# Routing tokens to experts: one threshold ahead of the experts, seven in steps between their matmuls

## The chip, the cores and the metric

The kernel runs on one core of one Trainium2 chip. The metric is the device time of one launch in microseconds (us), the median of the runs. The core has five engines with queues of their own, each working through its instructions in order: PE (TensorE, matmul, with its weight loads shown as PEld), DVE (VectorE), ACT (ScalarE), POOL (GpSimd) and SP (which here only issues DMAs). An engine waits for another only through semaphores.

## The reference, cut to what matters

The reference is two transformer layers over 4096 tokens of width 256. The last block, a mixture of eight experts, is the one that matters here. Each expert chooses its own tokens: the 1024 with the highest scores.

```python
n = b * l                                   # 4096 tokens
k = min(max(int(n * C / e), 1), n)          # 1024 of them for each of e = 8 experts
S = jax.nn.sigmoid(xt @ Wg).T               # scores, expert by token
G, I = jax.lax.top_k(S, k)
ex = xt[I]
hid = jax.nn.gelu(jnp.einsum('ekh,ehf->ekf', ex, W1) + b1[:, None, :], approximate=False)
out = (jnp.einsum('ekf,efh->ekh', hid, W2) + b2[:, None, :]) * G[..., None]
new_x = jnp.zeros_like(xt).at[I.reshape(-1)].add(out.reshape(-1, h))
```

Here `e` is 8, `h` 256 and the hidden width 1024. The input `xt` is a layernorm of what the attention block before it leaves, and a layernorm of `new_x` is added to that at the end.

## The kernel before, in words

The kernel runs four stages in turn: a gated attention layer with its feed forward, a 16-head attention with ReLU weights, the routing, and the experts. In all stages the order of PE, DVE and ACT work is written out by hand (`manual_schedule`); POOL and SP are ordered by the framework until expert 6, from where POOL is by hand too.

**The end of the attention.** The last two tiles of 128 tokens are closed by `at_once` (L1249 to L1278), a chain of small steps on DVE: output projection, three layernorms, the transposes for the router (`turn_gating`, L1203) and the router matmul (`gate`, L1216), whose result is added to `logits` (L1233). `logits` has 128 partitions, 16 segments of 256 tokens by 8 experts, and 256 columns, the tokens of a segment. Loops of matmuls on nothing (`keep_busy`, L203) stand where PE would otherwise be idle.

**The routing (L1462 to L1564).** The sigmoid of all logits is taken at once (L1468 to L1471). Two transposes and eight DMAs put the scores beside the tokens' rows in DRAM (L1478 to L1486, `tok_d`). Then all eight thresholds are searched together, bit by bit: 15 rounds of two bits each (L1497 to L1524). In a round, DVE compares the 256 scores of a partition with three candidates and counts (L1501, with an accumulator), one small matmul adds the counts of an expert's segments (L1505), and three short DVE steps choose the next candidates (L1509, L1516, L1520). From the thresholds a mask, a tie rule and two running sums give every chosen token its place in its expert's list (L1527 to L1564): the chunk `hi` and the place in the chunk `lo`.

**The lists (class `List`).** For an expert, `chunks` (L1577) and four `places` (L1591) turn `hi` and `lo` into zero-one matrices on DVE, four `collect` (L1601, eight matmuls each) multiply them to the list of token numbers, and `gather` (L1615) folds it to indices and issues eight indirect DMAs on POOL (`fetch`, L1626) that bring the rows of the chosen tokens, 128 each.

**The experts (`feed_forward`, L1805).** Each expert is done in two units of 512 tokens, so u = 0 to 15. A unit has eight steps f (hidden blocks: matmuls L1819 and a gelu on ACT, L1826) and four steps i (output tiles: matmuls L1842, DVE steps L1859 and L1860, a scatter with addition on POOL, L1861). After i = 1 and i = 2 the next unit's tokens are transposed (`turn`, L1790, evacuated by DVE, L1803). Unit 0 does the f steps in two halves of 256 tokens. In the first unit of each expert the next expert's list is made: `chunks` after f = 1, `places` after f = 2 to 5, all four `collect` ahead of the i steps, and `gather` after i = 0. The list of expert 0 is made ahead of unit 0 (L1874 to L1880), and 15 empty matmuls follow its `gather`.

## Time and profile before

| what | us |
|---|---|
| median of 3 runs (1625.87 to 1626.36) | 1626.24 |
| the profiled execution, its own time | 1625.33 |
| its span, first to last instruction | 1623.5 |
| PE busy | 1562.3 (96%) |
| DVE busy | 904.9 (56%) |
| ACT busy | 647.6 (40%) |
| POOL busy | 402.0 (25%) |
| attention and router end, last addition to `logits` | at 1089.5 |
| first round of the search to the threshold | 1093.3 to 1122.9 |
| first matmul of expert 0 | at 1141.8 |
| one unit of an expert without, with a list to make | 28.4, 30.7 |

"Busy" is time in which an engine worked on an instruction; a busy PE may be one that works on nothing (`keep_busy`). A row of the timeline has the start in us from the span's start, the duration, the engine, the line of the kernel, the operation, what it writes from what, the shape, and in brackets the idle time of the engine before it and what ended it. The chain of waits is followed back from the last instruction, at each step to what released it.

### The profile page before, as it was taken

The numbers are of one execution on the slowest core, as the hardware profiler recorded it, in microseconds if no ns is written. First come the engines' busy times: TensorE is split into PE (matmuls) and PEld (weight loads), VectorE is DVE, ScalarE is ACT, GpSimd is POOL, SyncE is SP. The second block draws the span as 40 slices with busy tenths as digits, with TensorE's granted clock in tenths as the row PEclk, the third lists the DMA queues.
The fourth block names the chain that finished last, engine by engine and source line by source line (L and its number), as shares of the span: only waits on it lengthen the run. The fifth ranks groups of instructions, "written<-read, shape, count | busy, mean of one in ns | idle before, by whom it ended". The sixth has DMA issues, their size and how long they took to land.

```text
span 1623.5 us, 23583 instructions
## 1 busy us (share of the span) xinstructions
PE 1562.3 (96%) x9270; PEld 797.6 (49%) x9270; DVE 904.9 (56%) x2080; ACT 647.6 (40%) x1115; POOL 402.0 (25%) x436
## 2 busy tenths in 40 slices
PE   7999999999999999999999999983999999999997
PEld 3666666666322223232323224541757667566574
DVE  5555565664657787878787787767211212222145
ACT  3344444544544545454544455641221121211233
POOL 4122232222201011111101010110424324324555
PEclk9999999999999999999999999996999999999999
DMA  8300000000000000101010100031233233233355
GB/s 205 121 1 1 1 1 1 0 1 1 1 1 1 11 31 7 34 1 40 1 40 1 36 4 27 28 129 30 57 75 70 66 75 72 66 75 88 67 146 140
DMA packets 70090, 71.22 MB, mean 44 GB/s; under 512 B 23613, under 2 KB 62938, under 8 KB 69850
## 3 DMA queue, kind: packets, MB, share of 16 engines
q1 hardware_dynamic: 56096, 47.01, 9.4%
q0 software_dynamic: 13008, 21.77, 7.4%
q8 instruction: 73, 1.20, 0.3%
q10 hardware_dynamic: 874, 0.93, 0.2%
q14 instruction: 39, 0.32, 0.1%
HBM read 41.74 MB, written 27.95 MB: 43 GB/s over the span
## 4 chain that ended last, share of the span: by engine, by line
PE 92%; DVE 3%; issue 2%; POOL 1%; ACT 1%; DMA 0%; POOLq 0%; SPq 0%; ACTq 0%; DVEq 0%
PE sc L1303 17%; PE po L1329 16%; PE ph L1819 13%; PE py L1842 13%; PE py L799 4%; PE pg L691 4%; PE pv L707 3%; PE ph L855 2%; PE po L771 2%; PE pt L1145 2%; PE pv L380 2%; PE pq L356 2%; PE pq L876 2%; PE po L775 2%; PE pk L356 2%
## 5 line engine op out<-in xcount | busy, mean ns | idle before, releaser
L1312 ACT ACTIVATE w<-sc 128x512 f32<-128x512 f32 x512 | 277.9, 594 | 218.5 <-PE sc L1303 101.7
L1317 DVE TENSOR_SCALAR w<-sc 128x1024 f32<-128x1024 f32 x240 | 293.2, 1222 | 99.2 <-PE sc L1303 71.1
L1303 PE MATMUL sc<-qT,kT 32*128 32x512 f32 (+1 forms) x2304 | 294.7, 586 | 1.5 <-ACT w L1312 0.8
L1329 PE MATMUL po<-w,vaug 128*17 128x512 f32 (+1 forms) x2304 | 276.1, 550 | 1.0 <-ACT w L1315 0.3
L1842 PE MATMUL py<-w,hid 128*128 128x256 f32 x1024 | 230.1, 380 | 0.0
L1826 ACT ACTIVATE hid<-ph,mb 128x512 f32<-128x512 f32 (+1 forms) x136 | 90.1, 662 | 344.4 <-PE ph L1819 343.7
L1819 PE MATMUL ph<-xT,w 128*128 128x512 f32 (+1 forms) x544 | 222.8, 567 | 0.7 <-DVE xT L1803 0.7
L1842 PEld LDWEIGHTS py<-w,hid 128*128 128x128 f32 x1024 | 191.1, 190 | 32.0 <-issue 7.0
L1303 PEld LDWEIGHTS sc<-qT,kT 32*128 32x128 f32 x2304 | 94.4, 183 | 173.9 <-issue 157.9
L1819 PEld LDWEIGHTS ph<-xT,w 128*128 128x128 f32 x544 | 103.2, 190 | 111.1 <-issue 107.6
L1329 PEld LDWEIGHTS po<-w,vaug 128*17 128x17 f32 x2304 | 44.8, 95 | 191.5 <-issue 157.5
L1861 POOL DMA_INDIRECT acc_d<-y,idx x56 | 88.2, 1574 | 156.1 <-issue 127.0
L1628 POOL DMA_INDIRECT got<-tok_d,idx x64 | 65.9, 1030 | 152.3 <-DVE idx L1618 135.2
L1859 DVE TENSOR_TENSOR y<-py,mb 128x256 f32<-128x256 f32 x56 | 23.4, 419 | 142.3 <-PE py L1842 135.9
L1803 DVE COPY xT<-tp 128x512 f32<-128x512 f32 (+1 forms) x34 | 22.3, 660 | 91.6 <-PE tp L1798 91.6
L1067 POOL TENSOR_TENSOR rsg<-veg,mhalf 128x1 f32<-128x1 f32 x30 | 16.7, 555 | 205.0 <-DVE veg L1066 205.0
L691 PE MATMUL pg<-nT,wh 128*128 128x512 f32 x128 | 60.8, 607 | 1.5 <-ACT nT L630 1.5
L799 PE MATMUL py<-wo,oT 128*128 128x256 f32 x256 | 61.9, 385 | 0.0
L707 PE MATMUL pv<-wh,nT 128*128 128x512 f32 x128 | 59.7, 592 | 0.0
L1618 DVE CAST idx<-parts 128x8 int32<-128x8 f32 x8 | 1.3, 167 | 101.8 <-PE parts L1616 101.8
L799 PEld LDWEIGHTS py<-wo,oT 128*128 128x128 f32 x256 | 47.3, 190 | 17.2 <-issue 9.4
L572 POOL TENSOR_TENSOR x<-x,y 128x1024 f32<-128x1024 f32 x14 | 32.9, 2351 | 73.3 <-ACT y L561 73.3
(295 smaller groups left out, 1933.3 us busy)
## 6 DMA issues: line engine op xcount, KB each, us to landing
w<-in_L_ffn_W_dram SPq DMA_DIRECT2D x16, 1024.0 KB, 5.2
x<-in_L_attn_x_dram SPq DMA_DIRECT2D x8, 512.0 KB, 4.0
acc_d<-logits SPq DMA_DIRECT2D x8, 512.0 KB, 5.1
tok_d<-hg SPq DMA_DIRECT2D x32, 128.0 KB, 1.7
x_d<-x SPq DMA_DIRECT2D x7, 512.0 KB, 2.9
back_w<-acc_d SPq DMA_DIRECT2D x6, 512.0 KB
out_dram<-x SPq DMA_DIRECT2D x20, 128.0 KB, 1.7
out_dram<-back_w POOLq DMA_DIRECT2D x4, 512.0 KB
```

The costliest lines, as they stand in the source:

```text
L691: nc.tensor.matmul(pg, lhsT=wh[:, c, HID + e * P : HID + (e + 1) * P], rhs=d["nT"][:, c, :], start=(c == 0), stop=(c == DC - 1),)
L707: nc.tensor.matmul(pv, lhsT=d["nT"][:, c, i * P : (i + 1) * P], rhs=wh[:, c, 0:HID], start=(c == 0), stop=(c == DC - 1),)
L799: nc.tensor.matmul(py, lhsT=d["oT"][:, e, :], rhs=wo[:, e, :], start=(e == 0), stop=(e == EC - 1))
L1303: nc.tensor.matmul(sc[:, m * n : (m + 1) * n], lhsT=row["kT"][t][rows, r, (kt + m) * P : (kt + m + 1) * P], rhs=row["qT"][rows, t, q0 : q0 ...
L1312: nc.scalar.activation(w[:, j, :], sc, AF.Relu)
L1317: nc.vector.tensor_scalar(w[:, 2:4, :], pair, 0.0, None, ALU.max)
L1329: nc.tensor.matmul(po[32 * j : 32 * j + HD + 1, weighed(halves, r)], lhsT=row["v"][:, kt + m, HQ * t + 2 * j + r, :], rhs=w[:, j, m * n : ...
L1628: return nc.gpsimd.indirect_dma_start(out=dst, out_offset=None, in_=rows[:, :], in_offset=self.at_chunk(c), bounds_check=NT - 1, oob_is_er ...
L1819: nc.tensor.matmul(ph, lhsT=w1[:, c, f * P : (f + 1) * P], rhs=xT[u][:, c, h * n : (h + 1) * n], start=(c == 0), stop=(c == DC - 1),)
L1826: nc.scalar.activation(hid[:, f, h * n : (h + 1) * n], ph, AF.Gelu, bias=mb1[:, e * FC + f : e * FC + f + 1])
L1842: nc.tensor.matmul(py, lhsT=hid[:, f, i * P : (i + 1) * P], rhs=w2[:, f, :], start=(f == 0), stop=(f == FC - 1),)
L1861: scatter = nc.gpsimd.indirect_dma_start(out=acc_d[:, :], out_offset=lists[e].at_chunk(k), in_=y, in_offset=None, bounds_check=NT - 1, oob ...
```

## The change

**Scores with tokens on partitions.** In `at_once`, ahead of the last router matmul, the logits of the first 30 tiles are transposed on PE, cut at -87 by DVE into `score_t` (128 partitions by 32 tiles by 8 experts, in the memory of `logits`), and their sigmoid is taken while the last tiles are still being normalized. One DMA stores those scores. The last router result is copied, transposed and made scores by itself, 16 columns wide, and stored by a second DMA.

**One search ahead, the others in steps.** A class `Search` holds the search for some experts at n bits a round. A `compare` is, per expert and candidate, one DVE comparison with accumulator over the 32 scores that a partition holds of that expert. A `tick` is the counting matmul (with a matrix of ones), the choice of the next candidates, and the next `compare`. Expert 0 is searched ahead of the experts at two bits (15 ticks). Experts 1, 2, (3, 4) and (5, 6, 7) are searched at three bits, 10 ticks each with 7 comparisons per expert.

**The places per expert.** `List.rank` takes the place of L1527 to L1564 for one expert: 13 short DVE steps and two matmuls, 32 or 64 columns wide.

**The order.** All steps of the searches and lists after the first stand in an agenda, each with the DVE time that it is reckoned to take and the earliest unit. After each f step and each i step of an expert one entry at most is issued, when what was issued before is reckoned to be done but for 0.3 us. Three entries (the first comparisons and two ticks of expert 1) are issued ahead of unit 0. `keep_busy` after the search and the lists goes from 13, 12 and 15 matmuls to 8 and 4; 13 behind the sigmoid are dropped.

```diff
@@ at_once
-                keep_busy(idle, 4)
+                tokens = side([P, SEG // P, P], "tokens")
+                for k in range(SEG // P):
+                    nc.tensor.transpose(tokens[:, k, :], logits[:, k * P : (k + 1) * P], ident)
+                keep_busy(idle, 3)
...
+                for k in range(SEG // P):
+                    nc.vector.tensor_scalar(
+                        score_t.rearrange("p (b z k) e -> p k z b e", b=B, k=SEG // P)[:, k],
+                        tokens[:, k, :].rearrange("p (z b e) -> p z b e", b=B, e=NE),
+                        -87.0, None, ALU.max,
+                    )
+                known = score_t[:, 0 : NTILE - SEG // P]
+                nc.scalar.activation(known, known, AF.Exp, scale=-1.0)
...
-                gate()
+                nc.vector.tensor_scalar(known, known, 1.0, None, ALU.add)
+                nc.vector.reciprocal(known, known)
+                score_rows = tok_d.rearrange("(j p) d -> p j d", p=P)[:, :, D : D + NE]
+                nc.sync.dma_start(score_rows[:, 0 : NTILE - SEG // P], known)
+                pg, rows = gate()
+                last_logits = wk.tile([P, SEG], F32, tag="y", name="last_logits")
+                nc.vector.tensor_copy(last_logits[rows, :], pg[rows, :])
...
+                new = score_t[:, NTILE - SEG // P : NTILE]
+                nc.vector.tensor_scalar(new, tokens[:, :, 32 - NE : 32], -87.0, None, ALU.max)
+                nc.scalar.activation(new, new, AF.Exp, scale=-1.0)
+                nc.vector.tensor_scalar(new, new, 1.0, None, ALU.add)
+                nc.vector.reciprocal(new, new)
+                nc.sync.dma_start(score_rows[:, NTILE - SEG // P : NTILE], new)
@@ class Search
+            def compare(self, r):
+                for i, e in enumerate(self.es):
+                    for k in range(1, self.v):
+                        ge = wk.tile([P, NTILE], F32, tag="ge", name="ge")
+                        nc.vector.tensor_scalar(
+                            ge, score_t[:, :, e], self.tried[:, i, k : k + 1], None, ALU.is_ge, ALU.add,
+                            accum_out=self.counts[:, r % 2, i, k : k + 1],
+                        )
+            def tick(self, r):
...
+                nc.tensor.matmul(pn, lhsT=all_b, rhs=counts, start=True, stop=True)
...
+                        nc.vector.scalar_tensor_tensor(kept, pn, float(TOPK), self.tried, ALU.is_ge, ALU.mult)
...
+                        nc.vector.tensor_reduce(best, kept, AX.X, ALU.max)
+                        nc.vector.tensor_tensor(
+                            tried.bitcast(I32),
+                            best.bitcast(I32).unsqueeze(2).to_broadcast([P, g, v]),
+                            now.unsqueeze(1).to_broadcast([P, g, v]),
+                            ALU.bitwise_or,
+                        )
...
+                    self.compare(r + 1)
...
+            def steps(self, behind=0):
+                g = len(self.es)
+                spent = 0.19 * g * (self.v - 1)
+                return [
+                    (spent, behind, lambda: self.compare(0)),
+                    *((spent + 0.6 + 0.1 * g, behind, lambda r=r: self.tick(r)) for r in range(self.rounds)),
+                ]
@@ class List
+            def steps(self):
+                behind = max(QPE * self.e - 3, 0)
+                return [
+                    (2.9, behind, self.rank),
+                    (1.2, behind, self.chunks),
+                    (1.4, behind, lambda: (self.places(0), self.places(1))),
+                    (1.4, behind, lambda: (self.places(2), self.collect(0), self.places(3), self.collect(1))),
+                    (0.3, behind, lambda: (self.collect(2), self.collect(3))),
+                    (0.3, behind + 1, self.gather),
+                ]
@@ feed_forward
-                    if coming is not None and h == TB // n - 1:
-                        if f == 1:
-                            coming.chunks()
-                        elif 2 <= f < 6:
-                            coming.places(f - 2)
+                    go_on_with_lists(u, 1.75 if u else 0.87)
...
+                go_on_with_lists(u, 1.9)
@@ ahead of the units
-        lists[0].chunks()
-        for part in range(4):
-            lists[0].places(part)
-            lists[0].collect(part)
-        lists[0].gather()
+        searches = [Search(*what) for what in (((0,), 2), ((1,), 3), ((2,), 3), ((3, 4), 3), ((5, 6, 7), 3))]
+        agenda = []
+        for search in searches[1:]:
+            agenda.extend(search.steps())
+            for e in search.es:
+                agenda.extend(lists[e].steps())
+        left = [0.0]
+        def go_on_with_lists(u, time):
+            left[0] = max(left[0] - time, 0.0)
+            if agenda and left[0] < 0.3 and agenda[0][1] <= u:
+                spent, _, step = agenda.pop(0)
+                left[0] += spent
+                step()
         first = ps.tile([P, TB], F32, tag="mm", name="idle", bufs=3)
-        keep_busy(first, 15)
+        for n, (_, _, step) in enumerate(searches[0].steps() + lists[0].steps()):
+            step()
+            if n == 0:
+                nc.vector.memset(parts[:, 0 : P + NC], 0.0)
+            if step == lists[0].rank:
+                keep_busy(first, 8)
+        for _ in range(3):
+            agenda.pop(0)[2]()
+        keep_busy(first, 4)
```

The constants made in the first stage (`later_constants`) change with it: about as many short DVE steps as before.

## The prediction

> **What bounds the kernel.** I read the chain of waits first: where is the end set, and does the routing lie on it? The page's shares say PE, and the chain in order of time says what a unit of an expert costs.
>
> ```profile
> PE 92%; DVE 3%; issue 2%; POOL 1%; ACT 1%; DMA 0%; POOLq 0%; SPq 0%; ACTq 0%; DVEq 0%
> ```
>
> ```profile
> 1187.60 6.91 PE py L1842 x32
> ...
> 1216.02 1.94 PE parts L1604 x30
> 1217.96 3.65 PE py L1842 x16
> 1221.62 3.56 PE py L1842 x16
> ```
>
> In the experts PE never waits, so every PE instruction put there costs its own time. Two output tiles take 6.91 us; with a list they take 3.65 + 3.56 = 7.21.
>
> Second, the timeline around the routing. Between the last addition to the logits and expert 0's first matmul, 52.2 us, PE has almost nothing real to do and DVE is the chain. The reader is to see the start-to-start times: comparison to comparison 0.40, round to round (1095.22 to 1097.18) 1.96, threshold to `chunks` 7.43, `chunks` to the first expert matmul 11.34.
>
> ```profile
> 1089.53 0.43 DVE L1233 TENSOR_TENSOR logits<-logits,pg 32x256 f32<-32x256 f32 x1 [2.37 <-PE pg L1224]
> ...
> 1093.27 0.48 DVE L1501 TENSOR_SCALAR_CACHE_REDUCE ge<-sc,bits 128x256 f32<-128x256 f32 x1
> ...
> 1095.22 0.48 DVE L1501 TENSOR_SCALAR_CACHE_REDUCE ge<-sc,tried 128x256 f32<-128x256 f32 x1
> 1095.63 0.08 DVE L1501 DVE_READ_ACCUMULATOR ge<-sc,tried 128x1 bf16 x1
> 1095.63 0.47 DVE L1501 TENSOR_SCALAR_CACHE_REDUCE ge<-sc,tried 128x256 f32<-128x256 f32 x1
> ...
> 1096.43 0.17 DVE L1509 TENSOR_TENSOR grown<-tried,bits 128x16 int32<-128x16 int32 x1
> 1096.57 0.16 PE L1505 MATMUL pn<-counts,same_b 128*128 128x4 bf16 x1 [1.79 <-DVE ge L1501]
> 1096.77 0.17 DVE L1516 SCALAR_TENSOR_TENSOR kept<-pn,grown 128x16 f32<-128x16 f32 x1 [0.17 <-PE pn L1505]
> 1096.98 0.17 DVE L1520 TENSOR_REDUCE tried<-kept 128x4 f32<-128x16 f32 x1
> 1097.18 0.48 DVE L1501 TENSOR_SCALAR_CACHE_REDUCE ge<-sc,tried 128x256 f32<-128x256 f32 x1
> ...
> 1122.99 0.48 DVE L1530 TENSOR_SCALAR_CACHE_REDUCE mask<-sc,thr 128x256 f32<-128x256 f32 x1
> ...
> 1130.42 0.43 DVE L1579 TENSOR_TENSOR which<-hi,count_c 128x256 bf16<-128x256 bf16 x1
> ...
> 1135.37 0.17 DVE L1618 CAST idx<-parts 128x8 int32<-128x8 f32 x1 [1.46 <-PE parts L1616]
> ```
>
> Third, the windows (window, length, busy time and count of PE, PEld, DVE, ACT, POOL, then granted clock): when does PE's clock fall, and how much room has DVE in a unit?
>
> ```profile
> 1094.00:1096.00 2.00, 0.16 (x1) 0.10 (x1) 1.76 (x10) 2.00 (x2) 0.00 (x0) 1.00 1.01 406
> 1096.00:1097.00 1.00, 0.16 (x1) 0.00 (x0) 0.80 (x7) 1.00 (x1) 0.00 (x0) 0.89 1.07 367
> 1097.00:1098.00 1.00, 0.00 (x0) 0.00 (x0) 0.96 (x6) 0.98 (x2) 0.00 (x0) 0.50 1.09 348
> 1174.00:1202.30 28.30, 28.30 (x105) 19.01 (x104) 4.44 (x10) 5.50 (x8) 9.07 (x6) 1.00 0.38 70
> ```
>
> DVE works 4.4 of a unit's 28.3 us, so the other searches fit beside the experts. The clock halves at about 1096.9, some 3 us after the last transposes (1093.8); a matmul of 0.16 us every 2 us doesn't hold it.
>
> **What goes from the path.**
>
> 1. Front. Before, 1089.53 to 1093.27 = 3.74 us. After: copy 0.42 (as L1233), two transposes with the waits around them 0.5 (0.41 for the pair at 1093.38), cut 0.2, exp 0.3 (0.42 for 256 columns, 0.20 for one), add 0.2, reciprocal 0.25 (a 128x16 one took that at 1075.88): 1.9. Gain 1.8. The rest of the sigmoid is covered: the two cuts (0.2 to 0.3 each) lie in DVE's 0.79 us wait for `pt` at 1077.86, add and reciprocal (0.29 + 1.75 x 240/256 = 1.9) in its 2.37 us wait before L1233. Uncovered, they cost at most those times. SP issued the eight score DMAs in 7.7 us (6.05 + 1.61), landing 6.3 us later; two DMAs with the same pieces start at about 1089 and are wanted by the first gather at about 1119. The weight loads behind them slip by up to 7.7 us, but `w1` of expert 0 was issued at 1079.3 and `w2` is wanted some 50 us later. Six small memsets go to POOL, idle for 50 us there. All that: nothing.
>
> 2. Search of expert 0. 45 comparisons are 32 wide instead of 256. A comparison's 0.403 us spacing is 256 elements at 0.96 GHz, 0.267, and 0.136 fixed. The slope is from rows: a 128x512 copy out of PSUM (L1803) takes 0.69, a 128x256 one 0.42, so 256 elements are 0.27. 32 wide gives 0.033 + 0.136 = 0.169. Gain 45 x 0.233 = 10.5. From both sides: 0.136 (length costs nothing) and 0.235 (a 128x1 step, 0.15, and the accumulator's reading, 0.085, one after the other). I take 0.17, by the same instruction's row. The Trainium skill, VectorE: DVE Perf Modes, section "The TRN2 errata", gives VectorE 58 cycles and the length at 0.96 GHz, 0.094 us for 32; by that the gain would be 13.9. The row of 0.40 for 256 (0.33 by the rule) says that the accumulator costs more.
>
> 3. Places. Before 7.43. `rank` is 13 DVE steps of 32 or 64 columns. The chain: two comparisons, to PE and back 0.58 (as 1123.39 to 1124.18, less the length), two scans 0.13 + 0.25 (0.68 for 256), then eight dependent steps at 0.2 (as 1122.60, 1122.79, 1122.99), one hidden beside another: 2.5. Gain 4.9.
>
> Sum of gains 17.2.
>
> **What comes onto the path.**
>
> 4. From `chunks` to the first expert matmul. The same DVE and PE steps, 11.34. New: behind `gather` (PE, 4.66 after `chunks`) seven comparisons, a tick, the matmul of a second tick, four empty matmuls, and only then the transposes of expert 0's tokens. 5.12 + 7 x 0.169 + 0.14 = 6.45; a tick of 2.1 (step 6) later the second tick's matmul, 8.6; four empty matmuls 0.9: 9.5, where the tokens landed at 9.2 in before. +0.15 to 0.4. The collects may still run at half clock (eight cold empty matmuls are 3.4 us, and it took 3.4 us at 1124.0 to 1127.4 to get the clock): up to +0.9. I take +0.9 in all, bounds 0 and 4 (the colder case is a rival).
>
> 5. PE instructions between the experts' matmuls. Nearest row for one small bf16 matmul there: L1616. Two lists' pairs of output tiles take 7.21 against 6.91; of the 0.30 about 0.1 falls to L1616 (3.56 against 3.46 for the pair behind it), 0.2 to leaving the block of collects. 38 ticks x 0.11 = 4.2, bounds 1 and 12.5 (0.03 each, or 0.33, the whole entry and exit of a block). Seven ranks, two adjacent matmuls, 0.14 each: 1.0. The collects of a list come in two blocks instead of one; a unit with a list takes 30.67 by the chain, without 28.43; less 0.11 for L1616 a block costs 2.13, of which 32 collects, four every 0.225 us, are 1.8; entry and exit are 0.33: 7 x 0.33 = 2.3. Sum 7.5.
>
> 6. Ticks that come too early. From a tick's matmul to the next of one expert, DVE needs 0.20 + 0.21 + 0.20 + 0.20 (three choosing steps, as 1096.57 to 1097.18 and one more) + 7 x 0.169 + 0.14 = 2.13. An f step gives 13.73/8 = 1.72, with the tick 1.83. The agenda books 2.03 and lets the next go when 0.3 is left, so of three f steps two carry a tick, and each second interval is 0.3 short: PE waits behind the tick's matmul, everything behind it too. Walking the agenda gives six such pairs (three in unit 0, one in 1, two in 2): 1.8. For two experts DVE needs 0.95 + 14 x 0.169 = 3.3 in 3.55, for three 4.5 in 5.3: no wait. Bounds 0 and 4.5.
>
> 7. Unit 0 between its halves. By the agenda a tick is issued after f = 7 of the first half, ahead of the copies (L1803) of the second half's transposes. They queue behind it on DVE: first copy done 2.0 + 0.42 after the tick's matmul, before 0.95 (1148.78 to 1149.73). +1.5.
>
> 8. The lists are gathered in units 1, 3, 5, 6, 9, 10, 12 instead of 0, 2, 4, and so on. POOL's eight fetches (1.32 apart) move behind the scatters of the unit before. Tightest is expert 3: `gather` about 14.5 us into unit 5, four rows landed 0.7 + 4 x 1.32 + 1.9 later, about 22, wanted at 23.4. No wait, margin 1.4.
>
> Costs 0.9 + 7.5 + 1.8 + 1.5 = 11.7. Net -5.5. On the profiled execution's own time, 1625.33 (span 1623.5), that is 1619.8; the median of the runs is 0.9 higher: **1620.7**.
>
> **The rivals.**
>
> A. *The clock is low when expert 0 starts.* After `gather` 15 empty matmuls are gone, and for 3.9 us PE has one tiny matmul. For it: the clock fell within some 3 us at 1096.9. Against: the four empty matmuls end the gap. Eight empty matmuls at half clock cost 0.9 more twice over, then up to 1.5 us of `ph`: +2 to +4 us, about 1624. The Trainium skill, TensorE: Matmul & The Clock Gate, section "Why this matters for your kernels", speaks against the change: no gaps over about 3 us, by which this gap would lose the clock and the sum would be this rival's. The rows agree with about 3 us; which side of the window's edge the gap falls on no row shows.
>
> B. *Slower: short comparisons don't shrink as reckoned.* Place: L1501's successor, on the path 45 times, and seven in each tick. At 0.235 the gains are 14.2, a tick needs 2.6 (six waits of 0.8, 4.6), two experts 4.2 for 3.55 (five of 0.7, 3.5), three 5.9 for 5.3 (four of 0.6, 2.4), step 7 is 2.0, with 7.5 and 1 from above 21.0: +6.8, 1633. It decides from about 0.20. For: no 32-wide comparison is in the trace. Against: the 256-wide row's fixed part is 0.136.
>
> C. *Each tick costs PE a block's switch,* 0.33: +8.4, 1629. For: the collects' rows. Against: L1616's.
>
> D. *Better hidden:* DVE keeps up and a tick slips in for 0.03: steps 6 and 7 partly gone, step 5 at 3.5 to 5: 1615.
>
> **How the numbers follow.** Forecast 0.44, A 0.19, B 0.14, C 0.10, D 0.13. A change of 0.2%, 3.3 us, is about what a measurement here can tell from none. Faster: the forecast (own range 1618 to 1623), D and a little of A: 0.59. Within: most of A, C: 0.27. Slower: B: 0.14. The range runs from D to C, 1614 to 1629, and leaves out B and the worst of D.
>
> **What would show it.** Comparison spacing 0.17 and round 1.29 in expert 0's search (step 2); search start to first `ph` about 34 us instead of 48.5; clock 1.00 at the first `ph` (A if 0.5); PE idle of about 0.3 us ended by a comparison in six places in units 0 to 2, and 1.5 us at L1803 in unit 0; units from 6 on without idle time. I am wrong if units 0 to 5 grow by more than about 10 us together, or if the last four units change.

## The result, and the profile after

| | before | after |
|---|---|---|
| median of the runs, us | 1626.3 (1625.87 to 1626.89, 4 runs) | 1638.99 (1637.57 to 1639.64, 4 runs) |
| ratio to before | | 1.0077 (95% interval 1.0059 to 1.0094) |
| profiled execution, us | 1625.33, span 1623.5 | 1637.57, span 1635.6 |
| search of expert 0, first comparison to the step behind the threshold, us | 29.7 | 20.3 |
| `chunks` to expert 0's first matmul, us | 11.34 | 13.09 |
| expert 0's first matmul at, us | 1141.76 | 1128.15 |

The change makes the kernel 0.8% slower; 1620.7 was predicted, so the prediction is wrong by 18 us and in sign. The front did what was said: expert 0 starts 13.6 us earlier. The sixteen units of the experts then take 25.7 us more than before (10.8 predicted), and the last three units and what follows them last as long as before.

First the chain of waits, as for before. The page could follow it over 17% of the span only (the sum of the shares; 99% before), so the shares say little. But in the experts DVE's comparisons now stand on it between PE's blocks, which before they never did:

```profile
PE 15%; DVE 1%; issue 1%; POOL 0%; DMA 0%; ACT 0%; POOLq 0%; DVEq 0%
```

```profile
1360.24 4.10 DVE ge L1500 x42
1364.56 5.25 PE ph L1859 x12
```

Then the timeline of the routing (start, length, engine, line). The reader is to see the spacing of comparisons, 0.19 (1091.87 to 1092.06; 0.169 predicted), and the three steps: search 1091.87 to 1112.19, `rank` 1112.19 to 1115.06 (2.87), `chunks` to the first `ph` 1115.06 to 1128.15.

```profile
1091.87 0.27 DVE L1500 TENSOR_SCALAR_CACHE_REDUCE ge<-logits,bits 128x32 f32<-128x32 f32 x1 [0.27 <-DVE logits L1288]
...
1092.06 0.26 DVE L1500 TENSOR_SCALAR_CACHE_REDUCE ge<-logits,bits 128x32 f32<-128x32 f32 x1
...
1112.19 0.41 DVE L1571 TENSOR_SCALAR kinds<-logits,thr 128x32 bf16<-128x32 f32 x2
...
1115.06 0.42 DVE L1607 TENSOR_TENSOR which<-hi,count_c 128x256 bf16<-128x256 bf16 x1
...
1128.15 1.13 PE L1859 MATMUL ph<-xT,w 128*128 128x256 f32 x4 [0.30 <-issue]
```

The windows of the same stretch (length, then busy time and count of PE, PEld, DVE, ACT, POOL, then granted clock) show rival A. The clock falls within the microsecond from 1120 (its mean there is 0.73) and is 0.50 from 1121 to 1127. The eight empty matmuls ahead of expert 0 took 1.87 and 1.81 us for four each, where 0.9 had been put down.

```profile
1120.00:1121.00 1.00, 0.00 (x0) 0.00 (x0) 1.00 (x10) 0.95 (x1) 0.00 (x0) 0.73 0.00 0
...
1121.00:1123.00 2.00, 0.17 (x1) 0.10 (x1) 1.64 (x16) 0.00 (x0) 1.63 (x2) 0.50 0.00 0
...
1125.00:1127.00 2.00, 2.00 (x7) 0.84 (x6) 1.04 (x12) 0.00 (x0) 1.39 (x3) 0.50 0.27 72
1127.00:1129.00 2.00, 1.70 (x9) 1.25 (x8) 0.76 (x2) 0.00 (x0) 1.66 (x2) 0.93 0.50 135
```

The costliest place is unit 6, 38.97 us long. Its timeline, PE, POOL and DVE together, gives a chain of four rows. Expert 4's `gather` runs on PE at 1324.49. The cast of its result to `idx` on DVE (L1659) comes only at 1334.15, 9.7 us later (DVE has then been idle for 13.22 us), and what ends the wait is a scatter, `acc_d<-y,idx`: the last of expert 2's scatters was issued at 1330.20. Behind the cast on DVE stand the 21 comparisons of experts 5, 6 and 7, and behind these, on PE, the tick at L1510 (6.76 us idle) with the whole expert network behind it.

```profile
1324.49 0.17 PE L1657 MATMUL parts<-fold,listed 128*128 128x8 bf16 x1
...
1330.20 1.56 POOL L1892 DMA_INDIRECT acc_d<-y,idx  x1 [3.03 <-issue]
1334.15 0.17 DVE L1659 CAST idx<-parts 128x8 int32<-128x8 f32 x1 [13.22 <-DMA acc_d<-y,idx]
...
1338.39 0.18 PE L1510 MATMUL parts<-counts,all_b 128*128 128x24 bf16 x1 [6.76 <-DVE ge L1500]
```

Before, expert 4's `gather` came in the same unit, but 19 us into it, 12 us after expert 2's last scatter was issued, and its cast followed at once:

```profile
1327.36 1.55 POOL L1861 DMA_INDIRECT acc_d<-y,idx  x1 [3.90 <-issue]
...
1339.68 0.17 PE L1616 MATMUL parts<-fold,listed 128*128 128x8 bf16 x1
1339.94 0.17 DVE L1618 CAST idx<-parts 128x8 int32<-128x8 f32 x1 [15.18 <-PE parts L1616]
```

In the changed kernel the wait costs more than its own length. The windows show the clock behind it at 0.50:

```profile
1331.50:1338.30 6.80, 0.13 (x1) 0.00 (x0) 4.15 (x43) 0.69 (x1) 3.35 (x4) 0.79 0.32 58
1338.30:1342.00 3.70, 3.60 (x6) 1.54 (x6) 3.33 (x34) 0.00 (x0) 2.79 (x4) 0.50 0.35 93
```

Without its idle time unit 6 is 32.2 us; in a later kernel that has no wait there it is 30.1. The difference, 2.1, is the slow clock.

The third place is `rank`. Its two `kinds` stand on DVE behind the `y` steps of the output tile before it, and its matmul stands on PE directly behind that tile, so PE waits for the `y` steps and both `kinds` on DVE: 1.82 us in unit 0 and, in the same way, 1.22 in unit 8.

```profile
1155.64 0.35 DVE L1891 TENSOR_SCALAR y<-y,got 128x256 f32<-128x256 f32 x1
1155.91 0.40 DVE L1571 TENSOR_SCALAR kinds<-logits,thr 128x32 bf16<-128x32 f32 x2
...
1156.36 0.19 PE L1573 MATMUL parts<-kinds,all_b 128*128 128x64 bf16 x1 [1.82 <-DVE kinds L1571]
```

The theory to test: the loss is made by waits on buffers and on DVE's order, not by the searches' own work. Rivals: the comparisons are too slow for their ticks (B), or the ticks cost PE a block's switch each (C).

### The profile page after: what moved, and what is told of

Same layout as the page of the kernel before. It is cut to its first block, busy times and chain, and to the rows that moved or that the text cites. A ratio compares the mean times of both kernels' runs of the same rounds, so it can differ in the third digit from the quotient of the medians.

```text
span 1635.6 us, 24811 instructions
## 1 busy us (share of the span) xinstructions
PE 1565.7 (96%) x9282; PEld 794.6 (49%) x9282; DVE 1023.0 (63%) x3268; ACT 649.2 (40%) x1116; POOL 402.5 (25%) x441
## 5 line engine op out<-in xcount | busy, mean ns | idle before, releaser
L1859 PE MATMUL ph<-xT,w 128*128 128x512 f32 (+1 forms) x544 | 233.2, 579 | 2.3 <-DVE xT L1844 2.0
L1500 DVE TENSOR_SCALAR_CACHE_REDUCE ge<-logits,tried 128x32 f32<-128x32 f32 x483 | 96.2, 267 | 2.8 <-DVE ge L1500 1.0
```

Source lines behind the costliest of these rows:

```text
L1500: nc.vector.tensor_scalar(ge, score_t[:, :, e], self.tried[:, i, k : k + 1], None, ALU.is_ge, ALU.add, accum_out=self.counts[:, r % 2, i, ...
L1859: nc.tensor.matmul(ph, lhsT=w1[:, c, f * P : (f + 1) * P], rhs=xT[u][:, c, h * n : (h + 1) * n], start=(c == 0), stop=(c == DC - 1),)
```

## The experiments

Unit lengths below are from the first `ph` of a unit to the first of the next; idle times are the waits that the trace notes at PE's instructions. Every kernel was timed beside the kernel before on the same chip, five rounds unless it is said otherwise. They ran on four chips, which turns out to matter.

**e_idx: eight buffers for the index lists.**

```diff
-                self.idx = wk.tile([P, NC], I32, tag="idx", name="idx")
+                self.idx = wk.tile([P, NC], I32, tag="idx", name="idx", bufs=NE)
```

> Changed kernel with eight buffers for the index lists instead of two, nothing else. Theory: PE's 6.77 us of idle time in unit 6 comes from a buffer. Expert 4's gather, now at the start of unit 6, must wait until expert 2's last scatter has read its list, because the two lists share a buffer; the 21 comparisons of experts 5 to 7 queue behind that cast on DVE, and the first tick's matmul behind them on PE. Then unit 6 falls from 38.97 to 32.2 us, the cast follows its matmul by less than 2 us, and the time falls by 6.8 us, to about 1632.2 (0.996 of the changed kernel). Rival: the three-expert comparisons themselves are too slow for the tick that waits for them (my rival B, 21 x 0.19 = 4.0 us against about 5 booked); then unit 6 keeps more than 3 us of idle time and the time falls by less than 3.5 us.

1631.53 us (1631.19 to 1632.79), ratio to before 1.0037 (1.0024 to 1.0051): 7.5 us less than the changed kernel. Unit 6 is 31.28 us long, 7.7 less. In its timeline the cast follows its matmul at once, and the tick has no wait:

```profile
1326.67 0.17 DVE L1659 CAST idx<-parts 128x8 int32<-128x8 f32 x1 [3.97 <-PE parts L1657]
...
1333.34 0.18 PE L1510 MATMUL parts<-counts,all_b 128*128 128x24 bf16 x1
```

The buffer is shown to be the cause; rival B isn't needed there, since the same 21 comparisons now end ahead of their tick. The gain is larger than the idle time of 6.76 because the clock stays up (1.00 in unit 6 from 1328 to 1338). New are two waits: unit 3's first tick, which waited 0.39 us, now waits 1.89, and unit 6 has one of 0.91 at an output tile. They come back below.

**e_kinds: `kinds` with the threshold.** The two comparisons move from the start of `rank` to the end of the last tick.

```diff
                         lists[e].thr = thr[:, i : i + 1]
+                        lists[e].sort_kinds()
...
+            def sort_kinds(self):
+                self.kinds = wk.tile([P, 2, NTILE], BF16, tag="kinds", name="kinds", bufs=4)
+                for v, op in enumerate((ALU.is_gt, ALU.is_equal)):
+                    nc.vector.tensor_scalar(self.kinds[:, v, :], self.scores, self.thr, None, op)
...
             def rank(self):
-                self.kinds = wk.tile([P, 2, NTILE], BF16, tag="kinds", name="kinds")
-                for v, op in enumerate((ALU.is_gt, ALU.is_equal)):
-                    nc.vector.tensor_scalar(self.kinds[:, v, :], self.scores, self.thr, None, op)
```

> Changed kernel in which the two comparisons that give rank's kinds are issued with the threshold, at the end of the last tick, and not at the start of rank one step later. Theory: PE idles 1.82 us in unit 0 and 1.22 us in unit 8 because rank's matmul stands directly behind an output tile on PE, while its kinds stand on DVE behind that tile's two y steps. Then both waits go and the time falls by about 3.0 us, to about 1636.0. Rival: the wait is for the threshold itself (the last tick's answer comes too late, 2.3 us after its matmul); then at least half of each wait stays, and the time falls by less than 1.5 us.

1636.33 us (1634.88 to 1637.45), ratio 1.0066 (1.0052 to 1.008): 2.7 less. Both waits are gone, in unit 0 as this row shows (no bracket behind it), and units 0 and 8 are 2.0 and 1.4 us shorter. As the theory had it.

```profile
1154.24 0.19 PE L1576 MATMUL parts<-kinds,all_b 128*128 128x64 bf16 x1
```

**e_half: unit 0's step behind the second half's copies.**

```diff
                     for c in range(DC):
                         turn(0, c, h)
+                    if h:
+                        go_on_with_lists(u, 0.87)
...
-                    go_on_with_lists(u, 1.75 if u else 0.87)
+                    if u or h or f < FC - 1:
+                        go_on_with_lists(u, 1.75 if u else 0.87)
```

> Changed kernel in which, in unit 0, the agenda's step that followed f = 7 of the first half comes after the transposes of the second half and their copies. Theory: the 1.97 us that PE idles at the second half's first matmul is the copies' wait behind a tick's comparisons on DVE; it returns to about 0.4 us, and the time falls by about 1.6 us, to 1637.4. Rival: the comparisons only move, and the next tick, now closer behind, waits longer: the 1.6 us come back at the ticks of unit 0, time within 0.5 us of the changed kernel.

1636.94 us (1636.29 to 1638.52), ratio 1.0073 (1.006 to 1.0087): 2.1 less. The first matmul of the second half waited 1.97 us, now 0.34, and unit 0 is 2.2 us shorter; nothing came back at its ticks. (In this trace units 3 and 6 are 0.8 us longer each.)

**e_warm: empty matmuls between the three entries ahead of expert 0.**

```diff
-        for _ in range(3):
-            agenda.pop(0)[2]()
-        keep_busy(first, 4)
+        for n in (7, 9, 4):
+            agenda.pop(0)[2]()
+            keep_busy(first, n)
```

> Changed kernel with 7 and 9 more empty matmuls between the three agenda entries ahead of expert 0, so that PE has no gap of over 0.5 us there. Theory (rival A of the prediction): the stretch from chunks to the first expert matmul took 13.09 us instead of 11.34 because the granted clock fell to 0.50 between gather and the transposes. With the gap filled the clock stays at 1.00 from 1121 to 1127, the stretch takes 11.3 to 11.6 us, and the time falls by 1.5 to 1.8 us, to about 1637.3. Rival: the stretch is set by the fetch of expert 0's rows and by the two ticks on DVE, not by the clock; then it stays at 13 us or gets longer by the empty matmuls, time same or up to 1 us more.

The clock and the stretch came as theory A said: granted clock 1.00 (the row below; 0.50 in the changed kernel), 11.42 us from `chunks` to the first `ph`, not 13.09. But the time is 1643.39 us (1641.18 to 1646.52, 4 runs), ratio 1.0116 (1.01 to 1.0131): 4.4 more. Neither the theory nor its rival had that. In the trace, 3.6 longer, expert 0 starts 2.1 us earlier, but units 0, 3 and 6 take 2.3, 1.4 and 0.9 more, and the span ends 1.1 later behind the last unit.

```profile
1121.00:1123.00 2.00, 1.88 (x11) 0.89 (x10) 1.64 (x16) 0.00 (x0) 1.69 (x2) 1.00 0.17 36
```

In unit 0 a tick's matmul runs at 1129.36 and DVE takes the answer up 3 us later, with nothing else to do in between; the tick after it then waits 1.82 us on PE.

```profile
1132.35 0.17 DVE L1531 SCALAR_TENSOR_TENSOR kept<-parts,tried 128x8 f32<-128x8 f32 x1 [3.04 <-PE ph L1859]
```

**e_fix3: the three helpful edits together.**

> Changed kernel with three of the edits together: eight index buffers, rank's kinds with the threshold, and unit 0's step after the second half's copies. Theory: three separate waits, so the gains add: measured alone 7.5, 2.7 and 2.1 us, together 12.3, from 1639.0 to 1626.7 us, which is the time of the kernel before (1625.9) within 0.1%. Rival: DVE and POOL are so full that a wait taken away comes back at the next tick (unit 3 grew by 0.8 to 1.5 us in each of the single edits); then the sum is 3 us or more short, 1629.7 or above.

1626.35 us (1624.32 to 1627.59), ratio 1.0006 (0.9997 to 1.0015): the gains add, 12.6 us where 12.3 were expected, and the change's loss is gone. Unit 3 still has a wait of 1.96 us (and unit 6 one of 1.03): DVE pauses several times between two comparisons, up to 0.94 us, and the trace names one of DVE's own comparisons as what ended each pause. These pauses are called late signals below; that a signal is what is late is a reading of the trace and wasn't tried by itself. The windows show what such a gap can cost besides: the clock falls behind it, though it is only 2 us long. The unit takes 34.10 us; without the idle time that is 32.1, where e_slim below, with no wait there, has 30.4. The slow clock cost 1.7.

```profile
1238.00:1240.00 2.00, 1.72 (x5) 0.84 (x5) 0.82 (x6) 0.00 (x0) 0.45 (x1) 0.88 0.37 112
1240.00:1242.00 2.00, 2.00 (x6) 1.20 (x5) 2.00 (x23) 0.69 (x1) 0.00 (x0) 0.50 0.09 14
```

**e_all: the three edits and the empty matmuls.**

> The three edits and the 16 empty matmuls between the entries ahead of expert 0. Alone these held the clock at 1.00 and brought expert 0's first matmul about 2 us forward, but the time rose by 4.4 us; 1.8 us of that is a tick in unit 0 whose answer DVE took up 3.0 us after the matmul, the rest small waits in units 3 and 6. Theory X: those waits are DVE's own pauses, which fall differently in every kernel; then the gain of the earlier start remains, 1624.5 to 1626, below the three edits by 1 to 2 us. Theory Y: expert 0 starting earlier itself makes DVE late in unit 0; then this is 2 to 5 us above the three edits, 1629 or more, with a wait of over 1 us at a tick of unit 0's first half.

1629.08 us (1626.24 to 1631.48), ratio 1.0019 (1.001 to 1.0028): what theory Y forecast. A tick in unit 0's first half is again answered 3.06 us late, and PE waits 1.50 us. That the earlier start makes DVE late is not shown by it: in e_rows_ge_warm below, on another chip, expert 0 starts earlier still and no tick waits over 0.15 us.

**e_dummy: tick matmuls that nothing waits for**, one run.

```diff
+        def more(u, kind):
+            for _ in range({(13, "f"): 1, (14, "f"): 2, (15, "i"): 1}.get((u, kind), 0)):
+                nc.tensor.matmul(
+                    parts[:, sums_at : sums_at + 8], lhsT=all_b, rhs=all_b[:, 0:8], start=True, stop=True
+                )
```

> Changed kernel with more tick matmuls (128x128 bf16 by 128x8) that nothing waits for: one after each of the eight hidden tiles of unit 13, two after each of unit 14, one after each of the four output tiles of unit 15. These units have no other guests and last 28.42, 28.42 and 27.71 us. It prices step 5. By my 0.11 a tick: unit 13 29.3, unit 14 30.2. By 0.167, what units 4 to 6 of the changed kernel suggest: 29.8, and 30.2 if a second one behind the first costs 0.03 to 0.05. By rival C, 0.33 for a block's switch: 31.1.

1642.78 us in its one run. Units 13, 14 and 15 take 29.32, 29.52 and 28.05 us: +0.90 for eight, +1.10 for eight pairs, +0.34 for four. One is 0.112 us, the second of a pair 0.025, one among `py` 0.085. Rival C is out, and 0.11 was right for the matmul alone. Six real ticks lengthen unit 4 of the changed kernel by 1.00 us, 0.167 each, without any noted wait. But in e_stride2 and e_rows below, whose comparisons come every 0.167 us and not 0.19, the same six lengthen it by 0.67, 0.112 each. So the matmul of a real tick costs what an extra one costs, and the other 0.055 are waits for DVE, too short to be noted: with two experts, DVE needs three choosing steps and 14 comparisons, and ticks come 3.64 us apart in the changed kernel (first two rows), where two f steps and a tick take 3.54 (last two rows, e_stride2).

```profile
1263.29 0.17 PE L1510 MATMUL parts<-counts,all_b 128*128 128x16 bf16 x1
...
1266.93 0.17 PE L1510 MATMUL parts<-counts,all_b 128*128 128x16 bf16 x1
```

```profile
1257.92 0.17 PE L1517 MATMUL parts<-counts,all_b 128*128 128x16 bf16 x1
...
1261.46 0.17 PE L1517 MATMUL parts<-counts,all_b 128*128 128x16 bf16 x1
```

**e_contig: expert 0's scores side by side**, one run.

```diff
+                    self.rows[0] = keep.tile([P, NTILE], F32, name="row0")
+                    nc.vector.tensor_copy(self.rows[0], score_t[:, :, 0])
```

> Changed kernel in which the search of expert 0 reads its 32 scores per partition from a tile of their own, not every eighth element of the logits; one copy of 32 columns is added. It prices step 2: comparison spacing was 0.19 us, 0.169 had been predicted. If the stride of 32 bytes is the reason, the spacing falls to about 0.17, the search by 45 x 0.02 = 0.9 us. If the fixed part of such an instruction is larger than the 256-wide row says, it stays 0.19.

1642.83 us in its one run. The spacing is 0.167 us in the search of expert 0, and a round 1.26 instead of 1.33: the stride is the reason, and the sum of step 2 holds for scores side by side. (The time is no less: in this run the gap between unit 0's halves and unit 6's wait were each followed by a slow clock, units 37.8 and 40.6 us.)

**e_rows, e_rows_ge, e_rows_ge_warm, e_direct: four on the three edits.** The first keeps all experts' scores side by side and, to make room, cuts five small tiles to one buffer and the index lists from eight to four; the second adds two scratch tiles; the third adds e_warm's empty matmuls; the fourth, without the layout and the smaller buffers, takes the rows of experts 1 to 7 by plain transfers, and leaves out the choice of rows.

```diff
+        rows = keep.tile([P, NE, NTILE], F32, name="rows")
+        nc.vector.tensor_copy(rows[:, 0, :], score_t[:, :, 0])
+        nc.scalar.copy(rows[:, 1:NE, :], score_t[:, :, 1:NE].rearrange("p j e -> p e j"))
...
-                        ge = wk.tile([P, NTILE], F32, tag="ge", name="ge")
+                        ge = wk.tile([P, NTILE], F32, tag="ge", name="ge", bufs=4)
...
-                    self.fetch(self.got[c], tok_d, c)
+                    if self.e:
+                        nc.sync.dma_start(self.got[c], tok_d[c * P : (c + 1) * P, :])
+                    else:
+                        self.fetch(self.got[c], tok_d, c)
```

> The three edits (1626.35 us) and, for all experts, scores copied once to a tile with an expert's 32 scores side by side (one copy of 32 columns on DVE ahead of the search, the rest on ACT); five small tiles get one buffer less to make room. Expert 0's search alone showed a comparison spacing of 0.167 us with such a tile, 0.19 without. Expected: search 45 x 0.023 = 1.0 us shorter, the copy 0.2 longer; a one-expert tick 2.12 us apart, not 2.28, so the five waits of 0.31 in units 0 to 2 fall to 0.15, 0.8 in all; 1624.5 to 1625.0. Rival: the ticks' waits are set by PE's own spacing and not by DVE's chain; then only the 0.8 of the search comes, 1625.5.

> As the one before, and the comparisons write four scratch tiles in turn, not two. A comparison waits for the last but one (same scratch tile). In unit 3 these waits end late: DVE's signals come 0.7 us apart for some microseconds, DVE pauses up to 0.94 us between two comparisons, and PE idles 1.96 us at that tick, after which the clock is 0.50 for 3 us. If the pauses add up through that wait, four tiles break the chain: unit 3's idle time falls below 1.2 us and the time by 0.5 to 2.5 us. If only the last signal, from the comparison to PE, is late, nothing changes: within 0.5 us of the one before.

> As the one before, and the 16 empty matmuls between the entries ahead of expert 0. Twice these held the clock, brought the first expert matmul 1 to 2 us forward, and gave more than that back to a tick in unit 0's first half, whose answer DVE took up 3.0 us after its matmul. If that late answer belongs to the place (the tick beside the last two of the eight fetches), it comes again: 1.5 to 3 us above the one before. If it is an accident of one order of instructions, it may be gone, 1 to 2 us below.

> The three edits (1626.35 us), and the rows of experts 1 to 7 come by plain transfers on SP's queue, of 128 rows in sequence each, not by POOL's fetch of the listed rows (the choice of rows is left out, the bytes are the same). It asks what makes signals late in units 3 and 6: they come late beside the last of POOL's eight fetches in every trace. If POOL's fetch is the cause, unit 3 loses its 1.96 us of idle time and the slow clock behind it, unit 6 its 1.03 (there POOL's queue holds the scatters that free y): time down by 3 to 4.5 us. If the rows' transfer itself is the cause, unit 3 keeps over 1 us, and the time falls by 1 us at most.

| run | us | ratio to before (95% interval) |
|---|---|---|
| e_rows | 1620.09 (1619.67 to 1621.15) | 0.9967 (0.9955 to 0.9979) |
| e_rows_ge | 1619.98 (1619.77 to 1621.52) | 0.9968 (0.9957 to 0.9979) |
| e_rows_ge_warm | 1619.09 (1618.79 to 1619.47) | 0.9961 (0.9947 to 0.9974) |
| e_direct | 1623.34 (1622.34 to 1624.2) | 0.9985 (0.9976 to 0.9994) |

e_rows gained 6.3 us against e_fix3, about four times what was expected. The one-expert ticks' waits fell from 0.31 to 0.15 as expected; the rest was that units 3 and 6 had lost their pauses. But e_direct, with the old stride, had lost them too, and these four ran on another chip than e_fix3. So what they say of the pauses was open, and e_direct decides nothing on POOL's fetch. Among the four: the scratch tiles do nothing here, and the empty matmuls now gain 0.9 us. They shorten the stretch from `chunks` to the first `ph` by 1.63 (12.98 to 11.35), expert 0's unit by 0.4, and 1.5 us are lost again behind the last unit, where the span ends 12.1 us after it, not 10.6; the chain ends in both with transfers to the output on POOL's queue.

**e_rows_only, e_slim, e_stride4, e_stride2: what of that is the layout.** e_rows_only is the changed kernel with e_rows' layout and one buffer for the five small tiles; its index lists keep their two. e_slim is the three edits with e_rows' smaller buffers and the old layout. The other two are e_slim with an expert's scores 16 bytes (`beside` is 4) and 8 bytes (2) apart; three rounds each.

```diff
+        beside = 4
+        apart = keep.tile([P, NE // beside, NTILE, beside], F32, name="apart")
+        rows = [apart[:, e // beside, :, e % beside] for e in range(NE)]
```

> The changed kernel with an expert's 32 scores side by side (and one buffer less for five small tiles), none of the other edits: the index lists keep their two buffers. If the stride of the scores is a cause by itself, the time falls by what it gave on top of the three edits, 6.3 us, less what the waits for the index list swallow in unit 6: 3.5 to 6.5 us, 1632.5 to 1635.5. Unit 6 keeps over 5 us of idle time at its first tick (the cast still waits for expert 2's last scatter), with no pauses between comparisons and no late signals beside POOL's fetches. If those 6.3 us came only with the other edits in place, the time falls by less than 2.5 us.

> The three edits and the one buffer less for listed, upto, place, chosen and part, with the scores as they were, every eighth element. A control: those buffers were cut only for room. Expected 1626.4, within 1 us of the three edits (1626.35), with the pauses in units 3 and 6. If it is near 1620, the cut buffers and not the layout gave the 6.3 us.

> The three edits, with four experts side by side in the score tile: an expert's scores lie 16 bytes apart, not 32 and not 4. Comparison spacing: 0.167 at 4 bytes, 0.19 at 32. An estimate from the page SBUF of the Trainium skill, section on cachelines (16 bytes; four fp32 may be strided for free), would have it at 0.167 up to 16 bytes if that rule bears on DVE's reads; if every element in a line of its own costs, 0.19 as at 32. Time 1620 by the first, 1626 by the second, and with it whether the late signals stay.

> The same with two experts side by side: scores 8 bytes apart. If the cost comes with the number of 16-byte lines, 0.167 to 0.18 here; if any stride costs, 0.19. Time between 1620 and 1626, with the spacing.

e_rows_only: 1636.18 (1633.14 to 1638.71), ratio 1.0063 (1.005 to 1.0077); above what was expected, since the 6.3 were not the layout's. Unit 6 keeps its wait for the index buffer (5.86 us, unit 37.63), unit 0 both of its own (1.80 each); behind the first of them the clock is 0.53 (1140 to 1142), and the unit takes 36.99, 1.3 more than in the changed kernel. e_slim: 1622.80 (1622.33 to 1623.97), ratio 0.9982 (0.9973 to 0.9991), neither 1626.4 nor 1620, and no pauses. e_stride4: 1623.76, 0.9984 (0.9975 to 0.9994); e_stride2: 1620.81, 0.9964 (0.9951 to 0.9978). Against e_slim on the same chip scores 8 bytes apart gain 2.0 us, about the 1.4 to 1.9 expected of the layout. Two timelines show where the step lies. From one comparison to the next it takes 0.20 in these rows at 16 bytes (0.19 in the median of 480) and 0.17 at 8.

```profile
1092.72 0.27 DVE L1507 TENSOR_SCALAR_CACHE_REDUCE ge<-apart,bits 128x32 f32<-128x32 f32 x1
...
1092.92 0.27 DVE L1507 TENSOR_SCALAR_CACHE_REDUCE ge<-apart,bits 128x32 f32<-128x32 f32 x1
```

```profile
1092.64 0.25 DVE L1507 TENSOR_SCALAR_CACHE_REDUCE ge<-apart,bits 128x32 f32<-128x32 f32 x1
...
1092.81 0.24 DVE L1507 TENSOR_SCALAR_CACHE_REDUCE ge<-apart,bits 128x32 f32<-128x32 f32 x1
```

**e_fix3_b, e_slim_b: is it the buffers or the chip?** The two kernels that differ in these buffers, unchanged, beside each other on one chip.

> The kernel with the three edits once more, beside the one with five buffers less, on one chip. So far all traces with late signals (the changed kernel, the single edits, the three edits) are from other chips than those without (the scores side by side, the plain transfers, the five buffers less). If the chip makes the late signals, this one may come without them: then units 3 and 6 have no pauses, and it lies within 0.5 us of the other, at about 1622.8. If the buffers make them, this is 1626.3 with 1.9 us of idle time in unit 3, and the other 1622.8 without.

> The three edits and the five buffers less, once more, beside the kernel without that cut: 1622.8 and no pauses in units 3 and 6 if the cut is what takes the late signals away; the same time as the kernel beside it, with or without pauses, if the chip decides.

1625.84 (1623.32 to 1627.04), ratio 1.0 (0.9991 to 1.0009), and 1625.63 (1623.73 to 1627.07), ratio 1.0 (0.9991 to 1.0009). Both have the pauses, so the buffers don't matter: the same kernel has them on one chip and not on another. This chip had shown them half an hour earlier too, in the single edits. The same instruction of the same kernel, first e_slim_b, then e_slim on the other chip:

```profile
1237.06 0.26 DVE L1500 TENSOR_SCALAR_CACHE_REDUCE ge<-logits,tried 128x32 f32<-128x32 f32 x1
...
1237.97 0.27 DVE L1500 TENSOR_SCALAR_CACHE_REDUCE ge<-logits,tried 128x32 f32<-128x32 f32 x1 [0.64 <-DVE ge L1500]
...
1239.41 0.17 PE L1510 MATMUL parts<-counts,all_b 128*128 128x16 bf16 x1 [1.79 <-DVE ge L1500]
```

```profile
1237.01 0.17 PE L1510 MATMUL parts<-counts,all_b 128*128 128x16 bf16 x1
```

## Why the prediction was wrong, step by step

The span of the profiled execution got 12.1 us longer, where 5.5 less was predicted: 17.6 us to account for. At 1639 the kernel is slower than every rival was priced (B, the slowest, at 1633), and no rival named the step that failed.

- **Step 8 is the step that failed.** It said of the lists gathered later "no wait, margin 1.4", and looked only at the side of the reader, whether expert 3's rows come in time (its figures add up to 22.4 against 23.4, a margin of 1.0). They did come in time. The list is also written, into one of two buffers, and the buffer's last reader is a scatter of two experts earlier, late in POOL's queue. Before, `gather` came late in unit 6, after those scatters; moved to the start of that unit it stands ahead of them. Idle 6.76 and 2.1 of slow clock: 8.9 in the profile, 7.5 by e_idx. Lists 6 and 7 met the same wait (their casts came 8.0 and 7.6 us after their matmuls) and cost PE nothing, since no tick stood behind them.
- **`rank` inside the experts was priced for its matmuls only** (step 5). The wait behind the `y` steps was not seen: 3.0 in the profile, 2.7 by e_kinds. Moving an instruction to another engine's order needs the queue on both engines.
- **Step 5, the size.** Predicted 7.5. The units of the changed kernel grew by 25.7, of which 14.2 is idle time and some 2.5 slow clock behind it (2.1 in unit 6, 0.4 in unit 0); that leaves 9.0. The tick's matmul was priced rightly: 0.112 (e_dummy, and unit 4 of e_rows), 4.3 for 38, where 4.2 was predicted. Some 1.0 are waits too short to be noted, which belong to step 6: units 3, 4, 7 and 8 are 0.2, 0.3, 0.2 and 0.3 longer than in e_rows, noted waits taken off. What is left, 3.7, is the lists, predicted 3.3.
- **Step 6.** Nine waits of 0.28 to 0.39, 2.9 in all; six, 1.8, predicted. The additional ones are in units 3, 7 and 8, at ticks of two and three experts. The dearer comparison is the cause of most: with 0.167 (e_rows) the waits of units 7 and 8 are gone, the 1.0 of short ones with them, and those of units 0 to 2 are 0.15. So the six waits came where they were forecast, but their size, 0.31 for 0.3, is luck: it was reckoned with 0.169, with which they are half as long. The one in unit 3 is a late signal (below).
- **Step 4 and rival A.** 13.09 us, +1.75; +0.9 predicted. The rival's mechanism came, below its price of 2 to 4 us on top of the forecast: 0.85 here and 0.4 in unit 0. The row is the clock of 0.50 from 1121 on; e_warm and e_rows_ge_warm confirm it: with the clock held the stretch is 1.7 and 1.6 us shorter. The Trainium skill, TensorE: Matmul & The Clock Gate, section "Why this matters for your kernels", asks for no idle gaps over about 3 us between bursts of matmuls. This trace doesn't agree with that length: the collects ended at 1119.2, a matmul of 0.18 us followed at 1119.7, and by 1121 the clock was 0.50.
- **Step 2 and rival B.** Search gained 9.4, predicted 10.5. Comparisons came every 0.19: not 0.169, and not the 0.20 from which B was to decide, though the waits of step 6 are B's mechanism at a smaller size. The fixed part and the slope were right, as e_contig shows with 0.167; what failed was that a row of 256 elements side by side was taken for 32 that lie 32 bytes apart.
- **Steps 1, 3 and 7 were right.** Front gain 1.7 (1.8), places 4.6 (4.9), the copies' wait 1.58 (1.5). The path to expert 0, 36.3 us from the first comparison, is 12.2 shorter than before, where 34 us had been given as the sign.
- **The signs of being wrong came.** Units 0 to 5 grew by 13.0 us together (more than 10 was to show an error), and units 6 and 8 have idle time of 6.76 and 1.5. Of the last four units, three are as before, and unit 12 is 2.1 shorter, as the list once made in it is now collected in unit 11.

Together, measured less predicted: 8.9 for step 8, 3.0 for `rank`, 0.5 for step 5, 2.05 for step 6, 0.85 for step 4, 0.1 for step 7, 1.5 for steps 1 to 3, 0.3 for a front that began later in this execution, and 0.4 of slow clock in unit 0: 17.6.

The late signals are in the changed kernel's trace too (its ticks pause near 1241 and 1343). What they are worth there wasn't measured; by e_slim_b against e_slim it is 2.8 us for the kernel with the three edits (1.8 in unit 3, 1.0 in unit 6). Why those chips have them stays open. On which chip the changed kernel's result was taken isn't on record, so the gains against it (7.5, 2.7 and 2.1) may hold some of the difference of chips; the traces show the same waits gone.

The best kernel, e_rows_ge_warm, is 0.39% faster than the one before (0.26 to 0.53). Its prices were mostly those of the prediction; what was missing was an index buffer, two instructions' place, and the layout.

## What to carry to other kernels

When a step moves earlier, ask who read last the buffer that it writes, and where that reader stands in its queue: not only whether the result comes in time. A wait on one engine costs another only if something that it needs stands behind it in order, so put a small step's inputs ahead of the large steps of the same engine, as `kinds` with its threshold. And price a stall with the clock that follows it: here 1.96 us of idle PE cost 1.7 more in one run, and 6.8 us cost 2.1 more.

## What the runs showed of the hardware

- **The stride of a comparison.** On DVE an accumulating comparison of 32 f32 values takes 0.167 us from one to the next at 4 and 8 bytes between values, 0.19 at 16 and 32. The Trainium skill, SBUF — State Buffer, section "Door 1: The DMA port swizzle", has a note on 16-byte lines, of which each needs two hits or more; that agrees with the step between 8 and 16. Its reading that four f32 may be stepped over for free doesn't: 16 bytes cost as much as 32.
- **Signals that come late on some chips.** On two of four chips every trace has three to six pauses of 0.1 to 1.0 us between two comparisons, around 1240 and 1343, beside the last two or three of POOL's eight fetches or up to 2.6 us behind them; on the other two there is none over 0.1. The kernel before has the same time on all four (1625.3 to 1626.0); its PE waits for DVE only 0.4 us in the experts. The kernel with the three edits, which hands small results from DVE to PE and back in every tick, lost 2.8 between one chip and another (e_slim_b, e_slim). Kernels should be compared within one chip; the 6.3 us of e_rows would have been put down to the layout otherwise.
- **A gap well below 3 us can lose the clock.** In unit 3 gaps of 1.96 us (e_fix3) and 1.89 (e_dummy) were followed by some 1.7 us of slow clock; gaps of 1.91 (e_kinds) and 1.89 (e_idx) at the same place weren't (1.00 in the windows behind them). So too in unit 0: behind a gap of 1.97 us the clock was 0.50 in e_contig and 1.00 in the changed kernel. So it isn't the length alone; what else decides wasn't tried.
- **The tail isn't all PE's.** 2.7 us that e_rows_ge_warm was ahead of e_rows_ge at the last unit's end became 1.2 at the end of the span.
